# Where the maxima of four context quarters meet: 32-partition copies on VectorE instead of two turns on TensorE

## Chip, core and metric

The kernel runs on one core of a Trainium2 chip. The metric is the device time of one execution in microseconds. The kernel before has a median of 1806.11 us over 3 runs (1801.5 to 1807.59).

## The reference, cut to what matters

Sixteen sequences of 56 tokens pass through four layers, each of which attends to a context of 1500 rows of 128. Layer 0 has one head, layers 1 and 3 have 16 heads with a mask on the context, layer 2 has causal attention among the tokens and then 16 small heads over the whole context. The part that the change touches is the softmax over the context in layers 1, 2 and 3:

```python
# layers 1 and 3
sim = einsum('bhid,bhjd->bhij', q, k)
sim = where(media_mask[:, None, None, :], sim, neg_inf)
out = einsum('bhij,bhjd->bhid', softmax(sim, axis=-1), v)
x = x + tanh(attn_gate) * (out @ Wo)
# layer 2, over the same context, without a mask
scores = einsum('bhqd,bhkd->bhqk', q * scale, k)
cctx = einsum('bhqk,bhkd->bhqd', softmax(scores), cv)
```

A softmax needs the maximum of each row of scores before its exponentials, or at least a shift that is common to the whole row.

## The kernel before, in words

**Units.** The context attention of layers 1, 2 and 3 is worked off in units. The context is cut into NQ = 4 quarters. A block of a unit is 32 rows (BW = 32: queries times heads) against all four quarters: `scores_block` makes four products, and quarter g lands on the partitions 32g to 32g+31 of one PSUM bank (`sc`, three banks). So one partition holds one row's scores of one quarter, and a row's four quarters lie on four partitions, 32 apart. A unit has n blocks. In layers 1 and 3 the mask of this input leaves only the last 384 context rows, and the program takes its short branch: n = 14, a quarter is 96 columns, five blocks share one bank (`each`), and a unit's blocks are masked by an addition (L350) and reduced to maxima (L354). In layer 2 a quarter is 375 columns, one block fills a bank, and one instruction (L344) copies the scores out and leaves the maximum; the four units of a sequence have n = 8, 8, 8 and 4. There are 64 units in layers 1 and 3 together and 64 in layer 2.

**The shift.** After the scores, `mx` (128 partitions, n columns) holds a maximum for each quarter of each row. The exponentials are taken per partition, so all four partitions of a row need one and the same shift. `shift_of(u, 0)` turns `mx` by a product with the identity into PSUM (L361, tile `t`, two buffers shared with other work), lets VectorE take the largest of the four quarters with its sign changed (L363, `nm`) and copy it to the other three places (L368). `shift_of(u, 1)` turns `nm` back by a second product (L373), and ScalarE copies the result into `shift` (through `scalar_copy`, L245).

**The other steps of a unit.** `weights_of` lets ScalarE take the exponentials of every block with `shift` as bias (L381), and reads out the sums. `turn_blocks` transposes the weights in 32x32 blocks on VectorE (L392). `sums` multiplies them with the context's values on TensorE (L795 in layers 1 and 3, L1131 in layer 2).

**Periods.** `period(u)` is one step of a pipeline of three units: it makes the scores of u, the shift and the transposes of the unit before (x) and the sums of the one before that (y). In layers 1 and 3 (`apart`) the order in the program is: the scores of u, a third of y's sums, a third of x's transposes, the first half of u's shift, a third of each, the second half of u's shift, the last thirds. The transposes are kept behind the instruction that the planner was last handed as `copied`, without a semaphore. In layer 2 a period has four parts of two score blocks and a quarter of y's sums; x's shift comes in the parts 0 and 1, its exponentials after part 1, its transposes in the parts 2 and 3.

**Order.** Every engine works off its own queue in order. What stands in which order in the queues is drawn up when the program is built: a planner takes, at each point of its own modelled time, the ready instruction that comes first in the program. So the order in the trace differs from that in the code: in layers 1 and 3 the products of L361 and L373 stand before and among the scores of the next unit.

**Work beside the periods.** `close` (layers 1 and 3) divides and projects the finished sums of two sequences (L732 to L757), `absorbed` makes the next queries (L702 to L713), `keys_queries`, `values` and `own_sums` (L1023 to L1080) serve layer 2, and once per group of four sequences `side` brings the remaining work of the layers before and after (projections, norms, feed-forward).

Of the kernel before, what the change touches and what calls it, by code (L numbers as in the profile page):

```python
# [9 lines left out]
F32 = mybir.dt.float32  # L10
# [6 lines left out]
ALU = mybir.AluOpType  # L17
AX = mybir.AxisListType
# [11 lines left out]
NQ, QW = 4, M // 4  # L30
NB, BW = 12, 32
# [5 lines left out]
US = 14  # L37
# [24 lines left out]
def tile_kernel(ctx: ExitStack, tc: tile.TileContext, a, layers=4, groups=NG):  # L62
# [3 lines left out]
    nc = tc.nc  # L66
# [9 lines left out]
    small = ctx.enter_context(tc.tile_pool(name="small", bufs=10))  # L76
# [5 lines left out]
    def psum(pool, tag):  # L82
        return pool.tile([128, 512], F32, tag=tag, name=tag)
# [8 lines left out]
    def turn():  # L92
        return psum(ps_t, "t")
# [4 lines left out]
    def few(w):  # L98
        return small.tile([128, w], F32, tag="few", bufs=8, name="few", padded_shape=[128, 16])
# [49 lines left out]
    def p_tile(name):  # L149
        return ppool.tile([128, UM * QB], F32, tag="p", name=name)  # L150
# [27 lines left out]
    ident = const.tile([128, 128], F32, name="ident")  # L178
# [65 lines left out]
    def scalar_copy(out, in_, scale=1.0):  # L244
        nc.scalar.activation(out, in_, AF.Copy, scale=scale)  # L245
# [84 lines left out]
    def scores_block(u, i):  # L330

        sc = psum(ps_s, "sc")
        w, each = u["w"], u["each"]
        some = range(i, min(i + each, u["n"]))
        for j in some:
            at = (j - i) * w
            for g in range(NQ):
                q, k = u["qk"](j, g)
                nc.tensor.matmul(  # L339
                    sc[g * BW : (g + 1) * BW, at : at + w], q, k, start=True, stop=True,  # L340
                    skip_group_check=True,
                )
        if each == 1:
            return nc.vector.tensor_tensor_reduce(  # L344
                u["p"][:, i, :w], sc[:, :w], u["mask"], 1.0, LOWEST,
                ALU.add, ALU.max, u["mx"][:, i : i + 1],
            ).ins.name
        m = len(some)
        p = u["p"][:, i : i + m]
        nc.vector.tensor_tensor(  # L350
            p, sc[:, : m * w].rearrange("p (i k) -> p i k", i=m),
            u["mask"].unsqueeze(1).to_broadcast([128, m, w]), ALU.add,
        )
        return nc.vector.tensor_reduce(u["mx"][:, i : i + m], p, AX.X, ALU.max).ins.name  # L354

    def shift_of(u, i):

        n = u["n"]
        if i == 0:
            u["t"] = turn()  # L360
            nc.tensor.transpose(u["t"][:n, :128], u["mx"], ident)  # L361
            nm = small.tile([128, 128], F32, tag="nm", bufs=1, name="nm")[:n]
            nc.vector.tensor_reduce(  # L363
                nm[:, :BW], u["t"][:n, :128].rearrange("k (g r) -> k r g", g=NQ), AX.X,
                ALU.max, negate=True,
            )
            u["nm"] = nm
            return nc.vector.tensor_copy(  # L368
                nm[:, BW:].rearrange("k (g r) -> k g r", r=BW),
                nm[:, :BW].unsqueeze(1).to_broadcast([n, NQ - 1, BW]),  # L370
            ).ins.name
        else:
            nc.tensor.transpose(  # L373
                u["t"][:, 128 : 128 + n], u["nm"], ident[:n, :n]
            )
            u["shift"] = few(n)
            scalar_copy(u["shift"], u["t"][:, 128 : 128 + n])

    def weights_of(u):
        for i in range(u["n"]):  # L380
            nc.scalar.activation(  # L381
                u["p"][:, i, : u["w"]], u["p"][:, i, : u["w"]], AF.Exp,
                bias=u["shift"][:, i : i + 1],
                accum_out=u["den"][:, i : i + 1],
            )

    def turn_blocks(u, lo, hi, copied=None):
        hi = min(hi, u["n"])
        if lo >= hi:
            return  # L390
        blocks = u["p"][:, lo:hi, :]
        turned = nc.vector.transpose(blocks, blocks)  # L392
        if copied:
            tc.add_manual_dep(
                turned.ins, copied,
                mybir.DependencyInfo(
                    mybir.DependencyClass.NoSync, mybir.DependencyReason.DATA
                ),
                reason="copies of scores go first",
            )  # L400
# [6 lines left out]
    def period(u):  # L407

        x, y = line["turn"], line["sum"]
        if u:  # L410
            n = u["n"]
            blocks = u["blocks"]
            u["p"] = p_tile("p")[:, : n * blocks * BW].rearrange("p (i k) -> p i k", i=n)
            u["mx"] = few(n)
            if u["w"] < blocks * BW:
                nc.gpsimd.memset(u["p"][:, :, u["w"] :], 0.0)
        if y:
            o = psum(ps_o, "o")
        if x and "shift" in x:
            weights_of(x)  # L420

        def sums(lo, hi):
            for j in range(lo, hi) if y else ():
                y["sum"](
                    o, y["p"][:, :, j * BW : (j + 1) * BW], j, start=j == 0,
                    stop=j == y["blocks"] - 1,
                )

        copied = None
        if u and u["apart"]:  # L430


            for i in range(0, n, u["each"]):
                copied = scores_block(u, i)
            if x and "shift" not in x:
                shift_of(x, 0)
                shift_of(x, 1)
                weights_of(x)
            at = y["blocks"] // 3 if y else 0
            sums(0, at)  # L440
            if x:
                turn_blocks(x, 0, x["n"] // 3, copied)
            copied = shift_of(u, 0)
            sums(at, 2 * at)
            if x:
                turn_blocks(x, x["n"] // 3, 2 * x["n"] // 3, copied)
            shift_of(u, 1)
            sums(2 * at, 3 * at)
            if x:
                turn_blocks(x, 2 * x["n"] // 3, x["n"], copied)  # L450
        else:

            for i in range(4):
                for j in range(2 * i, min(2 * i + 2, n)) if u else ():
                    scores_block(u, j)
                if y:
                    sums(i * y["blocks"] // 4, (i + 1) * y["blocks"] // 4)
                if x and i < 2 and "shift" not in x:
                    shift_of(x, i)
                    if i:  # L460
                        weights_of(x)
                if x and i > 1:
                    at = -(-x["n"] // 2)
                    turn_blocks(x, (i - 2) * at, (i - 1) * at)
        if y:
            y["out"](o)
        line["turn"], line["sum"] = u, x
# [250 lines left out]
    def att13(name, gi, state, then, side, ends, last):  # L718
# [46 lines left out]
        for n in range(per * G):  # L765
# [31 lines left out]
            def qk(i, g, k=k, q=qa[:, b % 2].rearrange("p n h -> p (n h)"), kt=kt):  # L797
                at, w = (k * ub + i) * BW, LW // 4 if short else QW
                return q[:, at : at + BW], kt[:, g * w : (g + 1) * w]

            period({
                "n": ub, "qk": qk, "mask": mask, "apart": True,
                "den": den[:, b % 2, k * ub : (k + 1) * ub], "sum": add, "out": out,
# [7 lines left out]
        if last:  # L811
            period(None)
            period(None)
# [427 lines left out]
    t = turn()  # L1241
# [129 lines left out]
```

## Time and profile before

| what | value |
|---|---|
| median of 3 runs | 1806.11 us |
| the profiled execution: time, and span from its first to its last instruction | 1809.23 us, 1807.4 us |
| granted TensorE clock, mean | 0.988 |
| window 175 to 460 us (layer 1): PE, DVE, ACT busy | 279.21, 193.71, 197.31 of 285 us |
| window 540 to 1425 us (layer 2): PE, DVE, ACT busy | 851.68, 588.87, 458.21 of 885 us |
| window 1425 to 1770 us (mostly layer 3): PE, DVE, ACT busy | 339.46, 214.10, 241.64 of 345 us |
| first turn L361, 128x128 out of n columns | 128 times, median 273 ns |
| second turn L373 | 128 times, median 227 ns |
| L363 and L368 on VectorE | 128 times each, medians 274 and 236 ns |
| ScalarE's copy to `shift` (L245, few from t) | 128 times, median 177 ns |

PE is TensorE, PEld its weight loads, DVE VectorE, ACT ScalarE, POOL GpSimd. The durations of single products overlap, so the room that one takes is read from the starts of its neighbours and from the chain of waits. In a line of the profile, "out<-in" names the tiles, and "<-PE t L361 14.3" after the idle time says what ended most of it.

### The profile page before, as it was taken

The page shows a single profiled execution, that of the slowest core. Times are in us where ns is not written, and L with a number is a line of the kernel's source. Part 1 is how long each engine was busy: PE and PEld are TensorE (multiplying, and loading weights), DVE is VectorE, ACT ScalarE, POOL GpSimd, SP SyncE. Part 2 cuts the span into 40 slices and gives each one's busy share as a digit, 9 for nine tenths or more (in the row PEclk, how much of TensorE's full clock was granted, in tenths as well). Part 3 has the DMA queues.
Part 4 walks back from the last instruction along what each step waited for, and adds up shares of the span by engine and source line. Part 5 has one row for each costly group of instructions (what it writes and reads, how often), then busy time and mean ns, then how long its engine had stood idle before and what let it go on. Part 6 is the DMA issues. An engine that isn't in the chain of part 4 may idle for free.

```text
span 1807.4 us, 55972 instructions
## 1 busy us (share of the span) xinstructions
PE 1700.8 (94%) x24156; PEld 1118.4 (62%) x24156; DVE 1120.4 (62%) x2726; ACT 1010.1 (56%) x3592; POOL 99.6 (6%) x222
## 2 busy tenths in 40 slices
PE   4888999999899999999999999999999999999997
PEld 2556677776574565555655556556655667777765
DVE  2344856667755757768467684676577646656662
ACT  1443967666544464635456354566455677666763
POOL 0000000000010000100001000010000000000000
PEclk9999999999999999999999999999999999999998
DMA  7431212120041030001210012102200031212120
GB/s 177 125 106 45 75 44 90 44 69 20 28 142 42 19 118 22 20 20 42 96 46 20 19 44 94 51 20 65 90 7 12 27 136 41 97 44 95 43 67 8
DMA packets 60135, 107.10 MB, mean 59 GB/s; under 512 B 7430, under 2 KB 44822, under 8 KB 59878
## 3 DMA queue, kind: packets, MB, share of 16 engines
q1 hardware_dynamic: 58726, 97.27, 16.8%
q0 software_dynamic: 1152, 6.14, 1.5%
q8 instruction: 192, 3.15, 0.7%
q14 instruction: 65, 0.53, 0.1%
HBM read 102.49 MB, written 0.92 MB: 57 GB/s over the span
## 4 chain that ended last, share of the span: by engine, by line
PE 75%; DVE 13%; ACT 6%; DMA 4%; issue 2%; POOL 1%; SPq 0%; DVEq 0%; ACTq 0%; POOLq 0%
PE sc L339 20%; PE o L795 8%; DVE p L392 5%; PE mm L1164 4%; ACT p L381 4%; PE o L1131 4%; PE mm L858 3%; PE mm L846 3%; PE mm L831 3%; PE t L1042 3%; PE mm L682 3%; PE t L702 2%; PE mm L1177 2%; DVE p L344 2%; PE t L743 2%; DMA x<-in_x 2%
## 5 line engine op out<-in xcount | busy, mean ns | idle before, releaser
L381 ACT ACTIVATE p<-p,few 128x96 f32<-128x96 f32 (+1 forms) x1344 | 588.3, 440 | 6.8
L339 PE MATMUL sc<-keys,qs 128*32 128x375 f32 x3584 | 403.9, 484 | 17.3 <-DVE few L344 17.2
L392 DVE STREAM_TRANSPOSE p<-p 128x480 f32<-128x480 f32 (+3 forms) x319 | 317.2, 1004 | 73.0 <-ACT p L381 71.6
L344 DVE CUSTOM_DVE_ANT_0 p<-sc,no_mask 128x375 f32<-128x375 f32 x448 | 235.1, 535 | 85.9 <-PE sc L339 72.7
L381 ACT ACTIVATION_READ_ACCUMULATOR p<-p,few 128x1 f32 x1344 | 252.3, 188 | 0.0
L339 PE MATMUL sc<-ktl,qa 128*32 128x96 f32 x7168 | 201.5, 249 | 3.7 <-DVE p L350 1.7
L339 PEld LDWEIGHTS sc<-keys,qs 128*32 128x32 f32 x3584 | 119.0, 109 | 124.2 <-issue 76.2
L1131 PEld LDWEIGHTS o<-p,vc 128*32 128x32 f32 x6144 | 138.5, 110 | 79.8 <-issue 58.4
L339 PEld LDWEIGHTS sc<-ktl,qa 128*32 128x32 f32 x7168 | 158.2, 110 | 35.5 <-issue 16.6
L795 PE MATMUL o<-p,kvl 128*128 128x448 f32 x384 | 169.1, 569 | 1.3 <-DVE p L392 1.3
L1131 PE MATMUL o<-p,vc 128*32 128x64 f32 (+1 forms) x6144 | 159.9, 215 | 5.8 <-DVE p L392 4.5
L245 ACT ACTIVATE few<-t 128x14 f32<-128x14 f32 (+2 forms) x128 | 22.4, 175 | 247.4 <-PE t L373 247.4
L350 DVE TENSOR_TENSOR p<-sc,mkl 128x480 f32<-128x480 f32 (+1 forms) x192 | 113.8, 608 | 27.9 <-PE sc L339 27.5
L354 DVE TENSOR_REDUCE few<-p 128x5 f32<-128x480 f32 (+1 forms) x192 | 114.4, 612 | 2.8
L795 PEld LDWEIGHTS o<-p,kvl 128*128 128x128 f32 x384 | 67.7, 193 | 56.5 <-issue 46.1
L1164 PE MATMUL mm<-xT,w 128*128 128x224 f32 (+1 forms) x384 | 80.8, 360 | 2.2 <-DMA w<-in_L_l_up 1.0
L1164 PEld LDWEIGHTS mm<-xT,w 128*128 128x128 f32 (+1 forms) x384 | 65.7, 178 | 19.1 <-DVE h2T L1169 4.4
L245 ACT ACTIVATE keys<-t 128x375 f32<-128x375 f32 x64 | 30.7, 480 | 63.6 <-PE t L1042 62.8
L245 ACT ACTIVATE ot<-o 128x448 f32<-128x448 f32 x64 | 33.8, 528 | 55.1 <-PE o L795 55.1
L702 PE MATMUL t<-qT,wl 64*128 64x112 f32 x512 | 56.0, 283 | 3.4 <-DVE qa L713 2.0
L831 PE MATMUL mm<-w,oT 128*112 128x256 f32 x256 | 57.6, 380 | 0.4 <-DVE oT L757 0.4
L702 PEld LDWEIGHTS t<-qT,wl 64*128 64x128 f32 x512 | 48.3, 187 | 14.1 <-DVE qa L713 3.9
(263 smaller groups left out, 2307.8 us busy)
## 6 DMA issues: line engine op xcount, KB each, us to landing
w<-in_L_W SPq DMA_DIRECT2D x16, 1024.0 KB
kt<-in_ctxT SPq DMA_DIRECT2D x16, 768.0 KB
w<-in_L_Wq SPq DMA_DIRECT2D x8, 1024.0 KB
w<-in_L_Wo SPq DMA_DIRECT2D x8, 1024.0 KB
ktl<-in_ctxT SPq DMA_DIRECT2D x32, 192.0 KB
kvl<-in_ctx_last SPq DMA_DIRECT2D x32, 192.0 KB
w<-in_L_v_qkv SPq DMA_DIRECT2D x4, 768.0 KB
w<-in_L_l_qkv SPq DMA_DIRECT2D x4, 768.0 KB
```

What stands on the lines that cost most here:

```text
L245: nc.scalar.activation(out, in_, AF.Copy, scale=scale)
L339: nc.tensor.matmul(sc[g * BW : (g + 1) * BW, at : at + w], q, k, start=True, stop=True, skip_group_check=True,)
L344: return nc.vector.tensor_tensor_reduce(u["p"][:, i, :w], sc[:, :w], u["mask"], 1.0, LOWEST, ALU.add, ALU.max, u["mx"][:, i : i + 1],).ins ...
L350: nc.vector.tensor_tensor(p, sc[:, : m * w].rearrange("p (i k) -> p i k", i=m), u["mask"].unsqueeze(1).to_broadcast([128, m, w]), ALU.add,)
L354: return nc.vector.tensor_reduce(u["mx"][:, i : i + m], p, AX.X, ALU.max).ins.name
L381: nc.scalar.activation(u["p"][:, i, : u["w"]], u["p"][:, i, : u["w"]], AF.Exp, bias=u["shift"][:, i : i + 1], accum_out=u["den"][:, i : i ...
L392: turned = nc.vector.transpose(blocks, blocks)
L702: nc.tensor.matmul(halves[e][:, j * TP : (j + 1) * TP], wkT[e * 64 : (e + 1) * 64, j0 + j, :], qT[e * 64 : (e + 1) * 64, j0 + j, tok], sta ...
L795: nc.tensor.matmul(o[:, : ub * BW], kv[:, j, :], p, start=start, stop=stop)
L831: nc.tensor.matmul(p[:TP, i * D : (i + 1) * D], oT[:, j, i * TP : (i + 1) * TP], wo[:, j, :], start=(j == 0), stop=(j == 7),)
L1131: nc.tensor.matmul(o[cols, : pieces * BW], made["v"][:, j, cols], p.rearrange("p (i g) r -> p g i r", g=4)[:, g], start=start, stop=stop, ...
L1164: nc.tensor.matmul(p[:w, k * T : (k + 1) * T], wt[:, c, cols], xe[n][:, c, :], start=(c == 0), stop=(c == 1),)
```

## The change

`mx` gets a middle index for the quarter: 128 partitions by four by n. The scores' maxima go to index 0 on all 128 partitions, as before. `shift_of` is now one function without a second half, all on VectorE and all in SBUF: three copies bring the maxima of the partitions 32 to 63, 64 to 95 and 96 to 127 to the indices 1, 2 and 3 of the first 32 partitions; one reduction over the four takes the largest, with its sign changed, into `shift` on the first 32 partitions; three more copies bring it to the other partitions. The products L361 and L373, the tile `t` for them, the tile `nm` and ScalarE's copy are gone. `mx` has a tag of its own with two buffers; before it was one of the eight buffers of `few`. In layers 1 and 3 the whole shift stands where its first half stood; in layer 2 the shift and the exponentials of x both follow part 0.

```diff
-                ALU.add, ALU.max, u["mx"][:, i : i + 1],
+                ALU.add, ALU.max, u["mx"][:, 0, i : i + 1],
...
-        return nc.vector.tensor_reduce(u["mx"][:, i : i + m], p, AX.X, ALU.max).ins.name
-
-    def shift_of(u, i):
-
-        n = u["n"]
-        if i == 0:
-            u["t"] = turn()
-            nc.tensor.transpose(u["t"][:n, :128], u["mx"], ident)
-            nm = small.tile([128, 128], F32, tag="nm", bufs=1, name="nm")[:n]
-            nc.vector.tensor_reduce(
-                nm[:, :BW], u["t"][:n, :128].rearrange("k (g r) -> k r g", g=NQ), AX.X,
-                ALU.max, negate=True,
-            )
-            u["nm"] = nm
-            return nc.vector.tensor_copy(
-                nm[:, BW:].rearrange("k (g r) -> k g r", r=BW),
-                nm[:, :BW].unsqueeze(1).to_broadcast([n, NQ - 1, BW]),
-            ).ins.name
-        else:
-            nc.tensor.transpose(
-                u["t"][:, 128 : 128 + n], u["nm"], ident[:n, :n]
-            )
-            u["shift"] = few(n)
-            scalar_copy(u["shift"], u["t"][:, 128 : 128 + n])
+        return nc.vector.tensor_reduce(u["mx"][:, 0, i : i + m], p, AX.X, ALU.max).ins.name
+
+    def shift_of(u):
+
+        n, mx = u["n"], u["mx"]
+        shift = u["shift"] = few(n)
+        for g in range(1, NQ):
+            nc.vector.tensor_copy(mx[:BW, g], mx[g * BW : (g + 1) * BW, 0])
+        nc.vector.tensor_reduce(
+            shift[:BW], mx[:BW].rearrange("p g i -> p i g"), AX.X, ALU.max, negate=True
+        )
+        for g in range(1, NQ):
+            last = nc.vector.tensor_copy(shift[g * BW : (g + 1) * BW], shift[:BW])
+        return last.ins.name
...
-            u["mx"] = few(n)
+            u["mx"] = small.tile(
+                [128, NQ, n], F32, tag="mx", bufs=2, name="mx", padded_shape=[128, NQ, US]
+            )
...
             if x and "shift" not in x:
-                shift_of(x, 0)
-                shift_of(x, 1)
+                shift_of(x)
                 weights_of(x)
...
-            copied = shift_of(u, 0)
+            copied = shift_of(u)
             sums(at, 2 * at)
             if x:
                 turn_blocks(x, x["n"] // 3, 2 * x["n"] // 3, copied)
-            shift_of(u, 1)
             sums(2 * at, 3 * at)
...
-                if x and i < 2 and "shift" not in x:
-                    shift_of(x, i)
-                    if i:
-                        weights_of(x)
+                if x and "shift" not in x:
+                    shift_of(x)
+                    weights_of(x)
```

## The prediction, made before the changed kernel ran

> **What bounds the kernel now.** I read the page's busy shares first, then its costliest groups, then the groups by shape for the lines that the change touches, then stretches of single stages with the chain of waits, the list of VectorE's instructions and the windows. First, the page and the groups:
>
> ```profile
> PE 1700.8 (94%) x24156; PEld 1118.4 (62%) x24156; DVE 1120.4 (62%) x2726; ACT 1010.1 (56%) x3592; POOL 99.6 (6%) x222
> L392 DVE STREAM_TRANSPOSE p<-p 128x480 f32<-128x480 f32 (+3 forms) x319 | 317.2, 1004 | 73.0 <-ACT p L381 71.6
> L344 DVE CUSTOM_DVE_ANT_0 p<-sc,no_mask 128x375 f32<-128x375 f32 x448 | 235.1, 535 | 85.9 <-PE sc L339 72.7
> L245 ACT ACTIVATE few<-t 128x14 f32<-128x14 f32 (+2 forms) x128 | 22.4, 175 | 247.4 <-PE t L373 247.4
> L363 DVE TENSOR_REDUCE nm<-t 14x32 f32<-14x128 f32 x64 | 17.3, 270 | 17.4 <-PE t L361 14.3 <-PE t L373 0.4
> L368 DVE COPY nm<-nm 14x96 f32<-14x96 f32 x64 | 14.5, 226 | 1.5
> ```
>
> TensorE looks like the bound and VectorE free at 62%. That is an average. An interval in layers 1 and 3 where only periods run (VectorE's list, then the windows: PE, PEld, DVE, ACT, POOL, clock, DMA):
>
> ```profile
> 1508.34 0.57 DVE L392 STREAM_TRANSPOSE p<-p 128x384 f32<-128x384 f32 x1
> 1508.98 0.28 DVE L363 TENSOR_REDUCE nm<-t 14x32 f32<-14x128 f32 x1
> 1509.29 0.24 DVE L368 COPY nm<-nm 14x96 f32<-14x96 f32 x1
> 1509.46 1.22 DVE L392 STREAM_TRANSPOSE p<-p 128x480 f32<-128x480 f32 x2
> 1510.62 0.61 DVE L350 TENSOR_TENSOR p<-sc,mkl 128x480 f32<-128x480 f32 x1
> ...
> 1510.62:1516.15 5.53, 5.51 (x132) 3.71 (x127) 5.39 (x13) 5.50 (x31) 0.00 (x0) 1.00 0.03 10
> ```
>
> L363 comes back every 5.53 us, and in it TensorE, VectorE and ScalarE are all full. TensorE's own need without the turns is 2.45 (112 score products, 1483.81 to 1486.26 in the chain) + 2.45 (six sums) = 4.90; the two turns and their waits cost 0.63. VectorE has no gap but 0.07 before L363.
>
> Layer 2 is different: where score periods run alone, a loop through ScalarE and VectorE sets the pace (chain of waits):
>
> ```profile
> 1166.29 2.48 ACT p L381 x8
> 1168.87 1.78 DVE p L392
> 1171.56 1.69 DVE p L392
> 1174.17 0.19 DVE nm L363
> 1174.36 0.46 DVE p L344
> 1174.82 0.18 DVE nm L368
> 1175.04 0.24 PE t L373
> 1175.31 0.19 ACT few L245
> 1175.57 2.48 ACT p L381 x8
> ```
>
> Exponentials, transposes, evictions, shift, the next exponentials: 9.28 us. Elsewhere in layer 2 (1190 to 1204) the chain is TensorE throughout and the turns stand in it at 0.20 (L361) and 0.15 (L373).
>
> [...]
>
> **The change part by part.** There are 128 units: 64 in layers 1 and 3 (n=14), 64 in layer 2 (n=8, 8, 8, 4).
>
> *Removed.* Per unit two turns on TensorE, L363 and L368 on VectorE, one ScalarE copy. Summed over the chain of the whole run these hold 18.0 (L361), 20.5 (L373), 5.2 (ScalarE's few), 3.5 (L363) and 1.8 us (L368): 49 us. L361 also waits 5.4 us (ten times) for a ScalarE copy to free a buffer of t; the maxima no longer take one of those two buffers. I count 4 of the 5.4.
>
> *Added.* Per unit seven small VectorE operations. No row has a 32x14 copy. From below: if copies overlap as L368 does, 0.08 each, a chain of 6x0.08 + 0.20 = 0.7. From above: 0.20 each (a 112x8 reciprocal, L905) plus a reduction at 0.25 and waits: 1.5. I take 0.155, the three-element floor of 0.147 plus some elements[...]; the reduction over 14x4 elements 0.20[...]; two dependent starts at 0.03, as between L363's end and L368. n=14: 6x0.155 + 0.20 + 0.06 = 1.19; n=8: 1.14. The 128 come to about 150 us where L363 and L368 had 56: VectorE goes from 1120 to about 1214.
>
> *Layers 1 and 3, full intervals.* From the first transposes to the second now takes 1.12 (1508.34 to 1509.46). Afterwards 0.57 + 1.19, and the held transposes start behind it: 1.73 to 1.76. So +0.61, and 5.53 becomes 6.14 on VectorE, while TensorE needs 4.90 and ScalarE 5.3. The starts of L363 show 30 such intervals (14 and 16): 30 x 0.61 = +18. TensorE's new idle 1.2 us per interval can take work of the next layer's projections early, where the planner sees the gap; it knows VectorE's load only by its own costs, so I give back a third: +12.
>
> *Layers 1 and 3, the other 34 units,* with close, absorbed or the side work in them: VectorE has 5 us of 14.5 free (9.29 busy in 1488.9 to 1503.4), TensorE is late, each saves 0.31 (0.11 + 0.20): -10.5. In the 16 closes the reciprocal L733, on the chain at 1520.33, may stand behind the copies: +0.2 each, +3. Sum -7.5.
>
> *Layer 2, TensorE-bound units.* ScalarE's few copy is on the chain for 25 of its 64 units; those are the loop turns. The other 39 save 0.35 each: -13.6. The copies come between two evictions L344; these go about 0.55 later. That is hidden by the three score buffers: the next block to need that buffer starts two blocks, about 1.4 us, later, and VectorE then idles 0.55 anyway (before 1192.75). Without that cover it would cost TensorE 0.5 per unit.
>
> *Layer 2, loop turns.* From L363 to the exponentials is 1.40 (1174.17 to 1175.57). Afterwards 1.14 + 0.1: -0.2 for 25 turns, -5. L392's wait for ScalarE (71.6 us in all) stays, since only the shift's latency shrinks. Two evictions that stood inside those 1.40 now stand behind the copies; VectorE then waits 2.70 us for ScalarE anyway. Weights are issued one step earlier in program order; ScalarE waited there, so nothing is pushed back but copies of keys and values, which have their own slack (0.6 to 1.6 us idle before each).
>
> The new wait is of the exponentials on the last copy instead of ScalarE's own copy. mx has two buffers instead of a share in eight: a unit's copies end before the unit after next writes. No DMA moves, nothing on SP's or POOL's queue.
>
> Sum: +12 - 7.5 - 13.6 - 5 - 4 = -18. Against the profiled execution (span 1807.4, time 1809.2): 1791. That execution is 3 us above the median of 1806.1, so I put the forecast at 1788.
>
> **The rivals.** 0.3%, 5.4 us, is what a measurement can tell from no change.
>
> *The copies overlap:* chain 0.7, VectorE as before, full intervals 0, the others -10.5, layer 2 -13.6 - 25 x 0.7 - 4. Total -46: 1760. For: L368's 0.17.[...] Chance 0.15.
>
> *A draw:* no fill, no relief by t, no gain in the loop: +18 - 7.5 - 13.6 = -3: 1803. For: it needs no luck. Chance 0.13.
>
> *Slower: VectorE becomes the bound.* One mechanism: seven operations in an in-order queue ahead of the evictions of scores and the transposes of weights that TensorE waits for. Price 150 us added against 53 (49 + 4) taken off the path; it decides once more than 35% of the added time lies on the path. My forecast has 23% there. In full intervals it is all there; if in layer 2 the planner lets the copies delay evictions in half of the units too, 45% are: 67 - 53 = +14, 1820. For: the full intervals, and TensorE already waits 44 us for L344 in layer 2 (17.2 + 27.2). Against: VectorE's 2 to 3 us of idle in each loop turn. Chance 0.27.
>
> *Forecast:* 0.45, its own range 1773 to 1800.
>
> **How the numbers follow.** Faster: forecast and overlap, 0.60; same: the draw, 0.13; slower: 0.27. The range reaches from near the overlap's 1760 to near the slower rival's 1820: 1762 to 1819.
>
> **What would show it.** Full intervals at 6.1 and VectorE at 1200 us or more: the price of the copies is right. Copies starting 0.08 apart: the overlap. 5.5 us intervals with TensorE full: fill by other work. In layer 2, turns of 9.1 instead of 9.28, and TensorE's wait for L344 still near 44 us; at 60 or more, the slower rival. I am wrong if layers 1 and 3 gain or layer 2 loses.

## The result, and the profile after

The changed kernel takes 1862.64 us (median of 4 runs, 1853.79 to 1865.68) against 1805.05 us (4 runs) of the kernel before on the same chip: 1.0307 times as long, with an interval of 1.0285 to 1.033. It is 58 us slower. The forecast was 1788 us, and the range ended at 1819.

The page of the changed kernel, its first line of busy times and the line of the chain that ended last:

```profile
PE 1652.9 (89%) x23900; PEld 1123.5 (60%) x23900; DVE 1249.8 (67%) x3366; ACT 1038.2 (56%) x3501; POOL 100.2 (5%) x222
PE 54%; DVE 32%; ACT 7%; DMA 4%; issue 2%; POOL 0%; SPq 0%; ACTq 0%; DVEq 0%; POOLq 0%
```

The chain line of the kernel before:

```profile
PE 75%; DVE 13%; ACT 6%; DMA 4%; issue 2%; POOL 1%; SPq 0%; DVEq 0%; ACTq 0%; POOLq 0%
```

VectorE's busy time grew by 129 us where I had written 94, TensorE's fell by 48. VectorE's share of the chain went from 13% to 32%. The profiled span went from 1807.4 to 1858.9, 51.5 us more. The mean granted clock of TensorE fell from 0.988 to 0.970.

The starts of the shift's reduction mark the units, 128 in each kernel. I cut the span at the first, the 28th, the 102nd and the last of them; the middle stretch holds layer 2 and the hand-overs on either side of it.

| stretch | before | after | difference |
|---|---|---|---|
| 1st to 28th shift (layer 1) | 296.4 | 314.2 | +17.8 |
| 28th to 102nd (layer 2) | 1012.8 | 1024.0 | +11.3 |
| 102nd to 128th (layer 3) | 274.9 | 301.0 | +26.1 |
| the rest of the span | 223.4 | 219.7 | -3.7 |

In the stretches of layers 1 and 3 there are 31 places where the interval from one shift to the next is a full one (5 to 7.3 us) in both kernels: they sum to 172.6 us before and 204.7 after. So of the 43.9 us that these two layers lost, 32.2 lie in full intervals and 11.7 in the 22 others.

One full interval of the changed kernel, in the list of VectorE's instructions (start, duration, then the group):

```profile
1634.67 0.57 DVE L382 STREAM_TRANSPOSE p<-p 128x384 f32<-128x384 f32 x1
1635.27 0.55 DVE L361 COPY mx<-mx 32x14 f32<-32x14 f32 x3
1635.86 0.23 DVE L362 TENSOR_REDUCE few<-mx 32x14 f32<-32x56 f32 x1
1636.13 0.55 DVE L366 COPY few<-few 32x14 f32<-32x14 f32 x3
1636.70 1.24 DVE L382 STREAM_TRANSPOSE p<-p 128x480 f32<-128x480 f32 x2
```

From the first transposes to the second it is now 2.03 us; before it was 1.12, and I had forecast 1.76. The shift itself, from the first copy to the transposes behind it, takes 1.43 where I had 1.19.

Windows of the changed kernel (after the length: PE, PEld, DVE, ACT and POOL busy, granted clock, DMA share, GB/s). The last one is a full interval, the first three belong to the close that comes below:

```profile
1611.00:1614.30 3.30, 1.39 (x27) 0.72 (x19) 3.13 (x8) 1.01 (x5) 1.76 (x2) 1.00 0.30 68
1614.30:1617.70 3.40, 3.40 (x17) 1.64 (x18) 2.77 (x6) 2.95 (x14) 0.14 (x1) 0.50 0.00 0
1617.70:1621.10 3.40, 3.40 (x31) 2.85 (x28) 2.04 (x4) 1.59 (x10) 0.00 (x0) 0.50 0.01 2
1635.86:1642.29 6.43, 4.96 (x130) 3.38 (x122) 6.19 (x17) 5.52 (x29) 0.00 (x0) 1.00 0.16 36
```

In the interval of 6.43 us VectorE is busy for 6.19, and the gaps of 0.01 to 0.04 around its small operations fill the rest. TensorE has 1.5 us free in it; over the 31 full intervals it is busy for 5.40 of 6.60 us in the mean, where it was busy for 5.54 of 5.57 before. VectorE is the bound, and room is left on TensorE.

The close that stands in those windows, TensorE's instructions after the change (in brackets what the engine waited for):

```profile
1610.33 1.32 PE L339 MATMUL sc<-ktl,qa 128*32 128x96 f32 x49
1613.56 2.79 PE L732 MATMUL t<-over,tables 32*128 32x448 f32 x4 [1.91 <-POOL over L726]
1616.75 3.26 PE L740 MATMUL t<-ot,wl 128*64 128x112 f32 x32
```

and a close of the kernel before:

```profile
1579.19 1.94 PE L743 MATMUL t<-over,tables 32*128 32x448 f32 x4 [0.41 <-POOL over L737]
1581.37 1.75 PE L751 MATMUL t<-ot,wl 128*64 128x112 f32 x32
```

The same 36 records take 6.05 us where they took 3.69. (They are 18 products of the program: each of these products stands twice in the trace.) The windows above say why: after a gap of 1.91 us the granted clock is 0.5 for 6.8 us. Of such stretches there are 24 in the changed kernel and 7 before, without one in each that outlasts the span. Over the 16 closes TensorE waits 19.3 us in front of these products, before 3.9. Counted in windows of one microsecond (TensorE's busy time by one minus the granted clock), 52.8 us of full speed are lost while TensorE is busy, against 19.1 before. This is called the lost time below. By the stretches of the table it went from 0 to 11.9 us in layer 1, from 10.2 to 25.0 in layer 2 and from 0 to 11.4 in layer 3. None of it lies in a full interval.

The third thing to see is copies that are held beside GpSimd. Two groups of the changed kernel that run at the same time, from its list of instructions:

```profile
1552.05 1.89 POOL L726 TENSOR_TENSOR over<-den,tables 32x448 f32<-32x448 f32 x2 [1.80 <-DVE den L722]
1552.62 1.56 DVE L366 COPY few<-few 32x14 f32<-32x14 f32 x3
```

Three copies that took 0.55 elsewhere take 1.56 beside GpSimd's products. The groups by shape give the mean of a copy in ns (second number after the bar):

```profile
L366 DVE COPY few<-few 32x14 f32<-32x14 f32 x192 | 47.8, 249 | 5.1
L361 DVE COPY mx<-mx 32x14 f32<-32x14 f32 x192 | 31.4, 164 | 4.7
```

The copies in take 164, the same copies out 249. I had no term for this, since GpSimd has only 100 us of work. Of the 768 copies 50 take over 0.3 us (0.41 to 0.94), and GpSimd is busy during every one of them; of the 702 copies during which it is idle, none takes over 0.17. The reductions L362 show nothing of the kind: 25 of the 128 run beside GpSimd, the longest of these for 0.235 us, against 0.242 among the others.

In layer 2 the held copies and the order in VectorE's queue meet. The chain of waits of the changed kernel there (start, duration, what):

```profile
1194.02 0.16 DVE mx L361
...
1194.59 0.55 DVE p L344
...
1195.26 0.46 DVE p L344
1195.75 0.47 DVE few L366
1196.25 0.62 DVE few L366
...
1197.14 2.48 ACT p L371 x8
```

From the first copy to the exponentials it is 3.12 us: two evictions of 1.0 us together come between the copies, and two copies are held to 0.47 and 0.62 beside GpSimd's products for the queries (L1025, which start at 1194.52). Ten microseconds earlier, without either, the same stretch took 1.46 (1183.57 to 1185.03). I had forecast 1.24. Of the 64 units of layer 2, 30 have evictions among their copies and 12 have copies held beside GpSimd. From the first copy to the end of the last they take 2.07 us in the mean where I had 1.14.

### The profile page after: what moved, and what is told of

It reads as the page before. It is cut to its first block, busy times and chain, and to the rows that moved or that the text cites. A ratio compares the mean times of both kernels' runs of the same rounds, so it can differ in the third digit from the quotient of the medians.

```text
span 1858.9 us, 56012 instructions
## 1 busy us (share of the span) xinstructions
PE 1652.9 (89%) x23900; PEld 1123.5 (60%) x23900; DVE 1249.8 (67%) x3366; ACT 1038.2 (56%) x3501; POOL 100.2 (5%) x222
## 4 chain that ended last, share of the span: by engine, by line
PE 54%; DVE 32%; ACT 7%; DMA 4%; issue 2%; POOL 0%; SPq 0%; ACTq 0%; DVEq 0%; POOLq 0%
PE sc L339 10%; DVE p L382 8%; ACT p L371 6%; DVE mx L354 4%; DVE p L350 4%; DVE p L344 4%; PE mm L1153 4%; PE mm L847 3%; DVE few L366 3%; PE mm L820 3%; PE mm L1166 3%; PE mm L671 3%; PE t L691 3%; PE mm L835 2%; DVE mx L361 2%
## 5 line engine op out<-in xcount | busy, mean ns | idle before, releaser
L339 PE MATMUL sc<-keys,qs 128*32 128x375 f32 x3584 | 409.6, 488 | 45.4 <-DVE mx L344 44.9
L344 DVE CUSTOM_DVE_ANT_0 p<-sc,no_mask 128x375 f32<-128x375 f32 x448 | 233.8, 539 | 78.1 <-PE sc L339 69.3
L339 PEld LDWEIGHTS sc<-keys,qs 128*32 128x32 f32 x3584 | 134.4, 110 | 139.5 <-DVE mx L344 68.9
L1120 PEld LDWEIGHTS o<-p,vc 128*32 128x32 f32 x6144 | 151.2, 111 | 80.0 <-issue 46.2
L339 PE MATMUL sc<-ktl,qa 128*32 128x96 f32 x7168 | 185.0, 248 | 1.9 <-DVE p L350 1.5
L339 PEld LDWEIGHTS sc<-ktl,qa 128*32 128x32 f32 x7168 | 153.9, 110 | 45.5 <-issue 19.7
L354 DVE TENSOR_REDUCE mx<-p 128x5 f32<-128x480 f32 (+1 forms) x192 | 114.1, 611 | 2.8
L366 DVE COPY few<-few 32x14 f32<-32x14 f32 (+2 forms) x384 | 85.9, 224 | 10.6
L245 ACT ACTIVATE sums<-o 128x64 f32<-128x64 f32 x64 | 13.4, 209 | 119.0 <-PE o L1120 110.7
L361 DVE COPY mx<-mx 32x14 f32<-32x14 f32 (+2 forms) x384 | 64.7, 169 | 10.1
L245 ACT ACTIVATE qa<-t 128x224 f32<-128x224 f32 x64 | 21.3, 361 | 74.4 <-PE t L691 74.1
## 6 DMA issues: line engine op xcount, KB each, us to landing
w<-in_L_W SPq DMA_DIRECT2D x16, 1024.0 KB
w<-in_L_Wq SPq DMA_DIRECT2D x8, 1024.0 KB
w<-in_L_Wo SPq DMA_DIRECT2D x8, 1024.0 KB
```

The source lines that it names most:

```text
L339: nc.tensor.matmul(sc[g * BW : (g + 1) * BW, at : at + w], q, k, start=True, stop=True, skip_group_check=True,)
L344: return nc.vector.tensor_tensor_reduce(u["p"][:, i, :w], sc[:, :w], u["mask"], 1.0, LOWEST, ALU.add, ALU.max, u["mx"][:, 0, i : i + 1],). ...
L354: return nc.vector.tensor_reduce(u["mx"][:, 0, i : i + m], p, AX.X, ALU.max).ins.name
L361: nc.vector.tensor_copy(mx[:BW, g], mx[g * BW : (g + 1) * BW, 0])
L366: last = nc.vector.tensor_copy(shift[g * BW : (g + 1) * BW], shift[:BW])
L1120: nc.tensor.matmul(o[cols, : pieces * BW], made["v"][:, j, cols], p.rearrange("p (i g) r -> p g i r", g=4)[:, g], start=start, stop=stop, ...
```

## The experiments

Theories at the start: A, VectorE's full queue in layers 1 and 3 is the loss; S, the copies held beside GpSimd; C, the order that the planner chose anew, to be seen in ScalarE's loads of function tables (87 before, 124 after). Later H was added: the half clock is a cost of its own. "Lost" is the lost time in the profiled run; L1, L2 and L3 are the three stretches of the first table.

| run | median us | ratio to before, interval | lost | L1 | L2 | L3 |
|---|---|---|---|---|---|---|
| before | 1805 to 1808 | 1 | 19.1 | 296.4 | 1012.8 | 274.9 |
| the change | 1862.64 | 1.0307 (1.0285 to 1.033) | 52.8 | 314.2 | 1024.0 | 301.0 |
| e1 | 1862.15 | 1.030 (1.0277 to 1.0324) | 63.8 | 322.9 | 1009.4 | 311.0 |
| e2 | 1805.15 | 0.9999 (0.9977 to 1.002) | 27.7 | 298.3 | 1011.7 | 275.0 |
| e3 | 1843.33 | 1.018 (1.0134 to 1.0226) | 63.4 | 316.4 | 1007.8 | 298.6 |
| e4 | 1755.66 | 0.9705 (0.966 to 0.975) | 41.9 | 302.0 | 952.6 | 285.7 |
| e5 | 1839.53 | 1.0178 (1.0154 to 1.0203) | 55.3 | 311.9 | 1015.5 | 290.9 |
| e6 | 1818.02 | 1.0069 (1.0043 to 1.0094) | 55.1 | 305.8 | 1000.5 | 289.1 |
| e7 | 1932.40 | 1.0675 (1.0639 to 1.0711) | 99.3 | 350.5 | 1027.7 | 333.7 |
| e8 | 1791.59 | 0.9909 (0.9881 to 0.9937) | 45.6 | 309.1 | 965.9 | 295.6 |
| e9 | 1922.67 | 1.0631 (1.0602 to 1.0661) | 74.5 | 347.5 | 1017.5 | 337.2 |
| e10 | 1788.12 | 0.9896 (0.9865 to 0.9926) | 22.0 | 300.2 | 989.7 | 276.4 |
| e11 | 1784.43 | 0.9873 (0.9842 to 0.9903) | 24.9 | 298.7 | 992.3 | 275.0 |
| e12 | 1742.32 | 0.9632 (0.9593 to 0.967) | 23.7 | 289.0 | 953.9 | 283.9 |
| e13 | 1879.87 | 1.0376 (1.0339 to 1.0413) | 74.9 | 326.8 | 1022.1 | 313.4 |
| e14 | 1783.19 | 0.9848 (0.9815 to 0.9881) | 23.7 | 297.0 | 992.7 | 277.5 |

### e1 and e2: the new shift in layers 1 and 3 alone, in layer 2 alone

`turned_shift` is the two-part `shift_of` of the kernel before. e1 keeps the two turns in layer 2:

```diff
-                if x and "shift" not in x:
-                    shift_of(x)
-                    weights_of(x)
+                if x and i < 2 and "shift" not in x:
+                    turned_shift(x, i)
+                    if i:
+                        weights_of(x)
```

e2 keeps them in layers 1 and 3:

```diff
-            copied = shift_of(u)
+            copied = turned_shift(u, 0)
...
+            turned_shift(u, 1)
             sums(2 * at, 3 * at)
```

> The new shift in layers 1 and 3 only, the turns in layer 2. Theory A (VectorE's queue is full where only periods run, so the longer shift lengthens every such interval, and the gaps that it opens on TensorE cost clock): the starts of the shift lag by 44 of the 52 us in layers 1 and 3, so about +44 us against before, full intervals 6.4 us. Rival B (VectorE's load as a whole, 129 us more, counts wherever it falls): half of it, about +26 us. Rival C (what costs is the other order of the queues, with 37 more table loads on ScalarE, most of them near layer 2): under +15 us.

> The turns in layers 1 and 3, the new shift in layer 2 only. Theory A: layer 2 took about 8 to 11 us of the 52, so +8 to +11 us, full intervals of layers 1 and 3 back at 5.53 us. Rival B: about +26 us. Rival C: +35 us or more, and most of the 37 additional table loads still there.

With layers 1 and 3 alone the whole loss is there; with layer 2 alone the time is that of before within 0.23%. So the loss comes with the new shift in layers 1 and 3, as theory A has it, though its sizes were missed: 54 us for e1 where 44 was written, nothing for e2 where it was 8 to 11. The order fell as a cause: e2 has 110 loads of tables, 23 more than before, at no cost, and e4 below has 121 and is faster than before. One sign that I had named turned out to say little: TensorE waits for the evictions L344 in e2 as long as in the changed kernel (114 us, against 44 before), and e2 is not slower.

e1 and the changed kernel also show what the half clock costs. In the stretch of layer 1 both have the same instructions in the same order on every engine (4080 records on TensorE, 581 on VectorE, 883 on ScalarE, 26 on GpSimd), and yet e1 takes 322.9 us there and the changed kernel 314.2. Of the 27 intervals 23 agree within 0.1 us. The other four:

| interval of layer 1 | the change | e1 | more time in e1 | more lost time in e1 |
|---|---|---|---|---|
| 10th | 27.83 | 30.46 | 2.63 | 3.41 |
| 14th | 17.34 | 20.28 | 2.95 | 5.12 |
| 18th | 27.85 | 29.12 | 1.28 | 1.43 |
| 26th | 22.36 | 23.95 | 1.59 | 1.71 |

The 10th holds a close. In the changed kernel:

```profile
258.28 1.94 PE L732 MATMUL t<-over,tables 32*128 32x448 f32 x4 [1.24 <-POOL over L726]
260.77 1.78 PE L740 MATMUL t<-ot,wl 128*64 128x112 f32 x32 [0.55 <-ACT over L245]
```

and in e1:

```profile
259.00 2.52 PE L756 MATMUL t<-over,tables 32*128 32x448 f32 x4 [1.24 <-DVE few L366]
261.50 3.25 PE L764 MATMUL t<-ot,wl 128*64 128x112 f32 x32
```

The wait is 1.24 us in both, though the profile names another releaser; once the clock stays, once it is halved. So the half clock has a price of its own in the changed kernel: 8.5 us of time for 11.7 of lost time, 0.7 of it.

Not settled: e1 and e2 don't add up stretch by stretch. Layer 2 has the same program in e2 and in the changed kernel and takes 12 us more in the latter. The planner's order differs between the two, and the lost time there is 18.4 us in e2 and 25.0 in the changed kernel, which can explain a part.

### e3: the six copies as reductions over one element

```diff
-            nc.vector.tensor_copy(mx[:BW, g], mx[g * BW : (g + 1) * BW, 0])
+            nc.vector.tensor_reduce(
+                mx[:BW, g], mx[g * BW : (g + 1) * BW, 0].unsqueeze(2), AX.X, ALU.max
+            )
```

and likewise for the copies out.

> The changed kernel with its six copies per unit written as reductions over one element. Theory S (copies of 0.6 to 0.9 us are copies that wait for an instruction of GpSimd that runs at the time): no such instruction over 0.3 us is left, VectorE's busy time falls by 20 to 30 us, and the time by 8 to 25 us against the changed kernel (1838 to 1855). Rival (a copy is long because its predecessor or its write is slow, whatever GpSimd does): lengths stay, no change within 5 us.

In the groups by shape of this run the copies out no longer differ from the copies in (156 ns):

```profile
L368 DVE TENSOR_REDUCE few<-few 32x14 f32<-32x14 f32 x192 | 30.5, 159 | 5.2
```

The time falls by 19 us and VectorE's busy time by 31 (20 to 30 written), as theory S has it, and none of the 768 reductions takes longer than 0.164 us. So in this form GpSimd holds none of them. Not all of the gain comes from that: a reduction is also 0.01 us shorter than a copy that nothing holds (0.156 and 0.159 in the mean for 32x14, against 0.164). The gain lies in layer 2, which falls from 1024.0 to 1007.8 us; layers 1 and 3 together take 615.0 against 615.2. Of the 25 us by which the long copies exceed a short one, 16 lie in layers 1 and 3, but the lost time there is 37.6 us in e3 and 23.3 in the changed kernel. Full intervals still take 6.4 us.

### e4 and e8: no copies, three copies

e4 leaves out the copies and the meeting of the quarters: each quarter shifts by its own maximum. e8 puts the three copies in back in the form of e3, read by nobody.

```diff
-        for g in range(1, NQ):
-            nc.vector.tensor_copy(mx[:BW, g], mx[g * BW : (g + 1) * BW, 0])
-        nc.vector.tensor_reduce(
-            shift[:BW], mx[:BW].rearrange("p g i -> p i g"), AX.X, ALU.max, negate=True
-        )
-        for g in range(1, NQ):
-            last = nc.vector.tensor_copy(shift[g * BW : (g + 1) * BW], shift[:BW])
-        return last.ins.name
+        return nc.vector.tensor_reduce(
+            shift, mx[:, :1].rearrange("p g i -> p i g"), AX.X, ALU.max, negate=True
+        ).ins.name
```

> The changed kernel without its six copies per unit: the shift is the maximum of the own quarter only, so the maximum over the four quarters is left out. Theory A: with one operation of 0.2 us in place of 1.45 us VectorE's full intervals fall to about 4.7 us and ScalarE's 5.3 us decide, TensorE's clock events go back to about seven, and the time lands below before, at 1760 to 1785. Rival C (order and table loads): still above before by 15 us or more.

> The version without copies (each quarter takes its own maximum, so the outputs differ) with three of the six copies back, as reductions over one element, read by nobody. Without copies 1756, with six in this form 1843. If VectorE's queue sets the pace throughout, half of the 87 us comes back: 1795 to 1803. If TensorE sets it up to a point and VectorE only beyond, under a third of it comes back: 1756 to 1785. If it is the chain of the six before the exps and not the busy time, the last three cost most and the time is likewise below 1785.

Without copies the time is 1755.66: taking the turns away is worth 52 us (of 1807.75), and the six copies cost 107. A full interval of e4, among its windows:

```profile
1449.93:1455.14 5.21, 5.21 (x146) 3.67 (x138) 5.11 (x11) 4.99 (x26) 0.00 (x0) 1.00 0.18 43
```

and one of e8:

```profile
1475.20:1481.12 5.92, 5.92 (x178) 4.38 (x171) 5.70 (x13) 5.82 (x30) 0.00 (x0) 1.00 0.16 41
```

In e4 TensorE is full and VectorE has 0.1 us left of 5.21. So there was never room for copies in this interval: three of them make it 5.9 us (e8), six make it 6.4 (e3 and the change), 0.20 to 0.24 us for each copy. In total the first three copies cost 36 us and the second three 52. At 1791.59 e8 lies between its expected ranges, 3 us below the first, and the stages differ. In layers 1 and 3 the first three copies cost 17 us and the second three 10, so VectorE's queue sets the pace there from the first copy on. In layer 2 they cost 13 and 42, so there the first three nearly hide.

The gain of e4 lies in layer 2 alone (1012.8 to 952.6). Layers 1 and 3 are 16 us slower than before, though their full intervals are faster by 0.3 us each; their lost time is 37.6 us, where the kernel before had none in them. That raised theory H.

### e7 and e9: four unread products in each close

To fill TensorE's gap before L732, four products of 32x448 were put into it. e9 lets them go over 128 partitions instead of 32, with the same columns.

```diff
             nc.vector.reciprocal(total[:BW], t[:BW, :N])
+            idle = turn()
+            for _ in range(4):
+                nc.tensor.matmul(
+                    idle[:, : 8 * N], m_half[:BW],
+                    ot[:BW, 0].rearrange("p h n -> p (h n)")[:, : 8 * N],
+                    start=True, stop=True,
+                )
             over = []
```

In e9 the operands are `ident` and `ot[:, 0]`.

> The changed kernel with four products added to each close (32x448, read by nobody), on TensorE between the sum's product and the product that waits for GpSimd; they do work that the reference doesn't ask for. If TensorE's half clock after its gaps is a cost of its own, the gaps in close shrink by some 2 us each, the full speed lost while busy falls from 53 us to 20 to 35 and the time to 1835 to 1855 in spite of 32 x 2 us of added work. If the half clock only fills time in which TensorE would wait for VectorE anyway, the time is 1860 to 1885.

> As the run with four unread products in each close, which took 1932 us and lost 99 us of full speed while busy, but the four go over 128 partitions in place of 32, with the same 448 columns. In that run the half clock came in whole windows of 3.41 us on one fixed grid, also after windows that TensorE had filled with products over 32 partitions. If a product over 32 partitions counts for less in what sets the clock, and the half clock lies on the path, the lost time falls to 40 to 70 us and the time with it, to 1880 to 1910. If the lost time falls and the time stays at 1925 to 1940, the half clock costs nothing here. If the lost time stays near 99, the number of partitions does not matter.

Both missed. In e7 the time rose by 70 us, 4.4 for each of 16 closes, somewhat more than four products of this shape take at full speed (3.9, since the two of L743 above take 1.94), and the lost time went up instead of down. In e9 the lost time is 25 us below that of e7, as I had expected of wider products, but it is above the 40 to 70 written; and the time is 10 us below, with ranges that overlap. The products added work on the path and cured nothing. The pair says something about the clock all the same (last section).

### e12 and e13: two unread products of the turns' shapes in each unit of layers 1 and 3

```diff
             copied = shift_of(u)
+            idle = turn()
+            nc.tensor.transpose(idle[:n, :128], ident[:, :n], ident)
...
+            nc.tensor.transpose(idle[:, 128 : 128 + n], ident[:n, :128], ident[:n, :n])
             sums(2 * at, 3 * at)
```

e12 adds them to e4, e13 to the changed kernel. They wait for nobody's data.

> The version without the six copies (each quarter shifts by its own maximum, which leaves out part of the computation) with two products of the turns' shapes put back in each unit of layers 1 and 3, read by nobody and waiting for nobody. The version without copies took 302.0 and 285.7 us in layers 1 and 3 against 296.4 and 274.9 of the kernel before, and lost 42 us of full speed while busy, against 19, nearly all in those layers. If TensorE's half clock after gaps is what layers 1 and 3 lose there, and the turns kept TensorE full, the two layers together fall from 588 to 565 to 578 in spite of some 0.3 us more work in each of 55 units, the lost time falls below 25 us, and the time is 1735 to 1750. If the half clock has nothing to do with it, the products cost what they take: the two layers rise to 595 to 606 and the time to 1762 to 1775.

> The changed kernel with two unread products of the turns' shapes in each unit of layers 1 and 3, waiting for nobody. It took 1862 us, 314.2 and 301.0 of them in layers 1 and 3, and lost 53 us of full speed while busy. If the half clock after gaps is a cost of its own here as it was in the version without copies, the lost time falls below 40 us, the two layers to 595 to 608 and the time to 1842 to 1856. If VectorE's queue paces these layers and the half clock only fills TensorE's waits, the two layers stay at 612 to 622 and the time at 1858 to 1870.

e12 came out as theory H has it: with 64 times two more products on TensorE the kernel is 13 us faster (the intervals of the two ratios overlap slightly), the lost time falls from 41.9 to 23.7 and layers 1 and 3 from 587.7 to 572.9. In layer 1 the lost time falls by 15.4 us and the time by 13.1, in layer 3 by 5.2 and 1.8. The planner drew up another order for e12, so the two products are not the only difference; the pair agrees with the comparison of e1 above, where the order is the same. TensorE's instructions in a close of e4:

```profile
1554.65 2.49 PE L727 MATMUL t<-over,tables 32*128 32x448 f32 x4 [1.82 <-POOL over L721]
1557.07 3.25 PE L735 MATMUL t<-ot,wl 128*64 128x112 f32 x32
```

and of e12:

```profile
1548.98 1.94 PE L730 MATMUL t<-over,tables 32*128 32x448 f32 x4 [0.51 <-POOL over L724]
1551.43 1.75 PE L738 MATMUL t<-ot,wl 128*64 128x112 f32 x32
```

A TensorE that comes later to the close waits 0.51 instead of 1.82 us there, and keeps the clock. Over the 16 closes it waits 8.8 us in place of 20.1. This suggests that the turns which the change took away had done one useful thing: they kept TensorE busy enough.

e13 missed both of its expectations. In the changed kernel the same products don't close the gaps (before L735, this run's product with GpSimd's result, TensorE still idles 17.7 us against 19.3), the lost time rises by 22 us and the time by 17. Where VectorE sets the pace, more work on TensorE was no cure here.

### e5, e6, e10, e11 and e14: the copies on other engines

e5 puts the six copies on GpSimd in layers 1 and 3, with turns in layer 2; e6 in all three layers. e10 has turns in layers 1 and 3 and GpSimd's copies in layer 2; e11 is e10 with the copies out on ScalarE; e14 is e11 with the copies in on VectorE in the form of e3. The edits are of one kind:

```diff
-            nc.vector.tensor_copy(mx[:BW, g], mx[g * BW : (g + 1) * BW, 0])
+            nc.gpsimd.tensor_copy(mx[:BW, g], mx[g * BW : (g + 1) * BW, 0])
...
-            last = nc.vector.tensor_copy(shift[g * BW : (g + 1) * BW], shift[:BW])
+            scalar_copy(shift[g * BW : (g + 1) * BW], shift[:BW])
```

> The six copies go to GpSimd in layers 1 and 3 (the reduction stays on VectorE), layer 2 keeps the turns by products. If the loss is VectorE's queue in layers 1 and 3 and nothing else of the change, the full intervals fall from 6.4 us to about 5.3 (those of the version without copies took 5.21) and the time is 1775 to 1795, below the kernel before. Rival: the copies on GpSimd are slow or keep VectorE's own copies waiting, the exps wait for them, and the time stays above 1810. Third: close's product of the sums waits behind the copies on GpSimd, TensorE's gaps there stay and the time is 1795 to 1815.

> The six copies go to GpSimd in all three layers. If layer 2 hides them as it hid VectorE's (putting the new shift in layer 2 alone moved the time by 0), this is within 6 us of the run with GpSimd in layers 1 and 3 alone. If in layer 2 the 400 ns of TensorE's turns count once VectorE is not loaded by copies, it is 8 to 15 us below it. If the queries' products on GpSimd are held up by the copies, it is above it.

> Turns by products in layers 1 and 3, and in layer 2 the new shift with its six copies on GpSimd. Between the 28th and the 102nd shift, the stretch of layer 2, the kernel before took 1012.8 us, the version without copies 952.6, the version with GpSimd in all layers 1000.5; in layers 1 and 3 all versions of the change took longer than the kernel before. If the stages add up, this is 12 us below the kernel before: 1790 to 1798. Rival: the 12 us come from what the layers hand to each other, and it is 1800 to 1808, no faster.

> As the run before it, with the three copies out on ScalarE, in its queue just ahead of the exps that read them, in place of GpSimd. If the hops between engines cost in layer 2 and ScalarE has the time there, it is 5 to 20 us below that run: 1775 to 1790. If ScalarE's 0.2 us a copy (0.6 us in each of 65 units) stands on the path, it is up to 30 us above it.

> Turns by products in layers 1 and 3; in layer 2 the copies in on VectorE as reductions over one element, the copies out on ScalarE, none on GpSimd. Layer 2 took 992 us with the copies in on GpSimd and out on ScalarE, 966 in the version with only the three copies in on VectorE, 953 without copies, 1013 before. If the hops to GpSimd and back cost more than VectorE's 0.6 us a unit, layer 2 takes 968 to 982 and the time is 1760 to 1776. If not, it takes 990 to 1010 and the time is 1784 to 1802.

e5 missed: 1839.53, not below 1795; its rival, a time above 1810, is what came. Full intervals take 5.7 us where I hoped for 5.3, and layers 1 and 3 are 32 us slower than with turns, with a lost time of 55 us. e6 is 22 us better than e5, more than expected, so layer 2 does profit from copies that leave VectorE. Groups of e6 by shape:

```profile
L366 POOL COPY few<-few 32x14 f32<-32x14 f32 x192 | 37.6, 196 | 29.4 <-DVE few L362 23.1
L362 DVE TENSOR_REDUCE few<-mx 32x14 f32<-32x56 f32 x64 | 15.0, 235 | 19.6 <-POOL mx L361 19.6
```

A copy costs GpSimd 0.19 to 0.20 us. VectorE idles 0.3 us before each reduction (19.6 us over 64), but most of that is the copies' own time: from the end of the last copy in to the start of the reduction it is 0.03 us in the median, and from the reduction's end to the first copy out 0.06.

e10, with each form where it does best, takes 1788.12, 2 us below the expected range, and is faster than the kernel before by 1%. e11 takes 1784.43, inside the expected 1775 to 1790, but only 4 us below e10 where 5 to 20 was written, and its interval overlaps with that of e10. e14 missed: I expected 1760 to 1776 from fewer ways between engines, and it takes 1783.19, with layer 2 at 992.7 as its alternative had it. The short ways measured in e6 agree with that. These three can't be told apart; each is 1.0 to 1.5% faster than the kernel before. Layer 2 takes about 990 us in all three, though it needs only 966 with three copies that nobody waits for (e8). The likely reason is that the exponentials wait for the whole chain of copies wherever these stand; no run takes it apart further.

## Why the prediction was wrong

Its own steps, with the time that each measured in the profiled executions:

| step | forecast | measured |
|---|---|---|
| full intervals of layers 1 and 3 | +18, less a third filled by other work: +12 | +32.2 |
| the other units of layers 1 and 3 (measured: the 22 intervals in their stretches) | -7.5 | +11.7 |
| layer 2, units and loop turns (measured: the middle stretch with its hand-overs) | -18.6 | +11.3 |
| `t` freed | -4 | can't be read alone; the rest of the span has -3.7 |

**The chain of copies was sized too small.** The direction of this step was right: VectorE is the bound of a full interval, and all that the chain adds lands in it. But I took 0.155 us a copy, 0.20 for the reduction and two gaps of 0.03, 1.19 together. The 0.155 was an estimate from the 0.147 of three elements reduced (L574 before), the 0.20 another, between that and the 0.222 of an operation over 128x56 (L931 before, in the mean). That each copy counts in full was my assumption; the trace of before has no such copy. Measured are 0.164, 0.23 and gaps of 0.21 in sum around the seven operations, 1.43. The gaps are the largest part of the difference. The increase per interval is 0.92 instead of 0.61, and 1.3 where the reciprocal of a close falls in as well (12 of the 31; before, none). That they count in full is what the trace of the changed kernel shows: none of the 768 copies starts before the operation ahead of it has ended (31 ns after it in the median), while 1761 of the 2469 operations of VectorE outside the shift do.

**Nothing filled the room.** I gave back a third of the loss for the next layer's projections. But the 31 full intervals took in only 38 records of later work (L252 and L820), and all of their 32.2 us of loss remain: nothing that I can see came back.

**The other units: a cost that was missing from the sum.** "TensorE is late, each saves 0.31" put the clock at nothing. With VectorE late and the turns gone, TensorE comes to 13 of the 16 closes before the result that it needs is there and waits 0.7 to 2.2 us. Around 10 of these 13 the clock is halved for 3.4 us or more. That this is a cost of its own is shown by e1 beside the changed kernel, where instructions and order are the same: 0.7 us of time for each microsecond of lost time. For the 23.3 us lost in layers 1 and 3 this gives an estimate of 17 of their 44 us. That is more than the 11.7 which the other units lost, so without the half clock they would have been somewhat faster than before, as I had forecast. The lost time of layer 2 is not priced by any run.

**Layer 2: hidden copies gained nothing.** "That is hidden by the three score buffers" and the saving of 0.35 in 39 units were both wrong in size. Taking the turns away is worth 60 us there (e4), three times the gain that I had written for it, and the copies eat all of it: evictions come between them, and GpSimd's queries hold them (16 of the 19 us of e3 lie in layer 2). The held copies are the second term that the sum did not have. Layer 2 alone is a draw (e2). How the copies' cost there divides among evictions, held copies and lost time stays open.

**The rival** "VectorE becomes the bound" named the right mechanism and had 0.27. It set the end at 1820 because it had the same small chain and neither the held copies nor the clock. Its 150 us for the seven operations of all units are 177 in the profile (64.7 copies in, 26.7 reductions, 85.9 copies out). Of these 177 the chain that ended last holds 111, or 63%, where the forecast had 23% and the rival 45%. Of the signs written down, VectorE's busy time over 1200 us and a loss in layer 2 came. TensorE's wait for L344 over 60 us came as well, at 114, but e2 has it without a loss.

## What to carry to other kernels

When three engines are full in the same interval, as here, price an edit that moves work between them by the engine that receives it, at its full start-to-start time, and give no credit for the room it leaves on the other unless the trace shows who will use it. Count small copies between partition groups in full: here one took 0.16 us in the median and began 0.03 us after the operation ahead had ended. Look at their place among evictions and beside GpSimd (up to 0.94 us for one copy here) before their number. Work taken off TensorE cost its clock here, 0.5 for 6.8 us behind a gap of 1.91: look at the windows behind each gap, not only at the gap.

## What the runs showed of the hardware

**The half clock lies on a fixed grid in these traces.** All 24 stretches of half clock in the changed kernel start at the same place of a grid of 3.413 us (within about 0.1 us), and last one, two or four of its cells. Take the cells at full clock in the changed kernel, from the first clock record at 30.5 us on: of those in which TensorE was busy for under 1.5 us, all 11 were followed by half clock; with 1.5 to 2.7 us, 12 of 84; with more, 1 of 407 (at 2.76). In all runs but e7 together these are 99 of 105, 135 of 867 and 17 of 6456. So gaps of 0.7 to 1.9 us in one cell of a busy stretch were sometimes enough, and the same wait of 1.24 us cost the clock in e1 and not in the changed kernel.

**Products over 32 partitions seemed to count for less.** In e7 half clock also followed 13 of the 414 cells that TensorE had filled for more than 2.7 us. All 13 are among the 19 such cells in which products over more than 32 partitions took under 1.5 us; of the other 395 none was followed by half clock. In e9, with the unread products over 128 partitions, it followed none of 414.

**A copy in another form was quicker.** A reduction over one element takes 0.147 to 0.159 us in the mean of its shape (e3), where the copy took 0.16 to 0.25, and none was held by GpSimd (the longest took 0.164).
